# Attention scores in blocks of 32 queries from two heads, with 32, 64, 96 and 128 keys, in place of blocks of 64 queries with 64 and 128 keys

## The chip, the cores and the metric

The kernel runs on one core of one Trainium2 chip. A core has five engines with queues of their own: TensorE (PE in the profile; its weight loads are listed apart as PEld), VectorE (DVE), ScalarE (ACT), GpSimd (POOL) and SyncE (SP, which here only starts DMAs). The metric is the device time of one execution in microseconds (us), median of three runs.

## The reference: what is computed

A residual multi-query attention layer over 64 batches of 128 tokens, 16 heads of 64, causal, with one extra null key whose score is a learned bias:

```python
xn = layernorm(x, g_in)
q = (xn @ Wq).reshape(b, n, H, DH).transpose(0, 2, 1, 3) * scale
kv = xn @ Wkv                      # one key and one value head for all 16
...
sim = jnp.einsum('bhid,bjd->bhij', q, k) + bias
sim = jnp.where(causal_mask, neg, sim)
sim = jnp.where(mask_p[:, None, None, :], sim, neg)
attn = jax.nn.softmax(sim, axis=-1)
out = jnp.einsum('bhij,bjd->bhid', attn, v)
out = layernorm(out.transpose(0, 2, 1, 3).reshape(b, n, INNER) @ Wo, g_out)
return x + out
```

Everything is fp32. Because of the causal mask, a block of 32 queries needs only the keys up to its own block: the four blocks of a batch need 32, 64, 96 and 128 keys.

## The kernel before

**Layout.** The 128 tokens of a batch are cut into four blocks of 32 (`Q = 32`). `PLACE = 0, 1, 3, 2` (L98) gives the order in which the blocks are stored: blocks 0 and 1 form the first half of the queries (`hf = 0`), blocks 3 and 2 the second (`hf = 1`). Eight chunks of the query projection hold 16 heads, two of 64 in each chunk's 128 rows: a head is named by `r` (upper or lower 64 rows), `u` (chunks 0 to 3 or 4 to 7) and `f` (0 to 3).

**Scores.** `scores(b, hf)` (L765) computes the scores of one batch and one half of its queries. For each `f`, `r` and `u` it issues one matmul on a quarter of the array: the 64 rows of `r` against 64 of the array's columns. The weights are the 64 queries of one head, the moving operand is `kT`, the keys: 64 keys for `hf = 0`, 128 for `hf = 1`. The result goes to PSUM partitions `u * 64` to `u * 64 + 63`, so `u` picks the column half of the array. That is 16 matmuls for each half, and four of them (two `r`, two `u`) run side by side. An fp32 matmul appears in the trace as two records, called passes here. Keys past the causal edge inside the 64 or 128 are computed too, and are masked by the bias.

**Bias and mask.** `biasp` holds the bias of all heads in the layout of the scores, with a very negative number above the diagonal (`load_bias` L203, `causal` L215, `null_shift` L232, all of them in the setup). `bias_add` (L738, POOL) makes a tile `s` of bias plus key mask for a batch one turn ahead; `scores_add` (L790, DVE) then adds the scores out of PSUM to it, one instruction for each PSUM tile; `scores_max`, `exps` (ACT), `rinv` and `scale` (POOL) make the softmax, and `blocks_T` (DVE) transposes it in blocks of 32 for the next product.

**Values.** `values(b)` (L891) multiplies the transposed blocks with the values: eight tiles of 32 rows by 64 columns run side by side, `s` picking the 32 rows and `r` the columns. For the rows named in `wide` two steps of 128 columns are joined into one of 256, so that the tiles of odd `s` issue other lengths than those of even `s`.

**Order.** The order of the instructions on each engine is that of the source (`manual_schedule`); waits between engines are set from the tiles that they share. After a setup of some 60 us the main loop works on a pair of batches in each turn, `a = 2d` and `b = 2d + 1`: `turn(d)` (L1092) for d = 1 to 29 issues the four score groups (a,0), (b,0), (a,1), (b,1), then on DVE the adds of (a,0) and (b,0), a maximum, and the adds of (a,1) and (b,1); on PE the values of the pair before follow. Their four PSUM rooms are `a`, `w`, `Y` and the other `w`, which the adds of (a,0) and (b,0) have to free first. Then `body` or `body_full` issues the projections, the output product and the norms. The last turns use `turn_end` and `body_end` (d = 30, 31) and `body_last`.

**Other places that hold queries.** `qT` tiles are written by the helpers from L471 to L725 (`q_copy`, `keep`, `q_out`, `keep_two`, `q_out_two`, `inner_out`); before, 64 queries of a head lie side by side in them.

Of the kernel before, what the change touches and what calls it, by code (L numbers as in the profile page):

```python
# [8 lines left out]
FP = mybir.dt.float32  # L9
# [8 lines left out]
def kernel(  # L18
# [59 lines left out]
    nc = tc.nc  # L78
# [124 lines left out]
    def load_bias(u):  # L203
        rows = slice(u * DH, (u + 1) * DH)
        bias_r = attn_bias.rearrange("(u f r) i j -> u r i f j", u=2, r=2)[u]
        for r in range(2):
            rf = slice(r * NF, (r + 1) * NF)
            nc.sync.dma_start(out=biasp[rows, rf, LK], in_=bias_r[r, 0:DH, :, 0:NL])
            for i, at in enumerate((N - Q, N - 2 * Q)):
                nc.sync.dma_start(  # L210
                    out=biasp[u * DH + i * Q : u * DH + (i + 1) * Q, rf, UK],
                    in_=bias_r[r, at : at + Q],
                )

    def causal(u):  # L215

        for rows, keys, base in (
            (slice(u * DH, (u + 1) * DH), LK, 0),
            (slice(u * DH, u * DH + Q), UK, N - Q),
            (slice(u * DH + Q, (u + 1) * DH), UK, N - 2 * Q),  # L220
        ):
            nc.gpsimd.affine_select(
                biasp[rows, :, keys],
                biasp[rows, :, keys],
                pattern=[[0, R8], [-1, keys.stop - keys.start]],
                compare_op=ALU.is_ge,
                fill=NEG,
                base=base,
                channel_multiplier=1,
            )  # L230

    def null_shift(u):  # L232

        rows = slice(u * DH, (u + 1) * DH)
        nc.vector.tensor_copy(
            nbp[rows].rearrange("p (r f) -> p r f", r=2),
            nbh[rows, u * R8 : (u + 1) * R8].rearrange("p (f r) -> p r f", r=2),
        )
        nc.vector.tensor_tensor(
            biasp[rows, :, 1 : ROW - 1],  # L240
            biasp[rows, :, 1 : ROW - 1],
            nbp[rows].unsqueeze(2).broadcast_to([DH, R8, NL + N]),
            ALU.subtract,
        )
# [11 lines left out]
    nc.gpsimd.memset(biasp[0:DH], 0.0)  # L256
    nc.gpsimd.memset(biasp[DH:, :, 0 : ROW : ROW - 1], 0.0)
# [213 lines left out]
    def q_tiles(g, j, tags):  # L471

        for h, tag in enumerate(tags):
            qT[g, j, h] = gp.tile(
                [P, 2, GB // 2, 2, 2, DH], FP, tag=tag, name=f"qT_{g}_{j}_{h}", bufs=1
            )
            q_tags[g, j, h] = tag
# [4 lines left out]
    def q_part(g, c, h):  # L482

        f = c % NF
        return qT[g, f // 2, h][:, f % 2, :, :, c // NF, :]

    def q_whole(g, j, u, h):
        return qT[g, j, h][:, :, :, :, u, :]
# [18 lines left out]
    def q_copy(pq, c, h):  # L507
        nc.scalar.copy(
            q_part(0, c, h), pq.rearrange("p t (h i) -> p t h i", h=2)
        )  # L510
# [68 lines left out]
    def keep(tag, g, f, name):  # L579
        u, h = KEPT[name]  # L580
        nc.scalar.copy(
            q_part(g, u + f, h), prod[tag].rearrange("p (t h i) -> p t h i", t=2, h=2)
        )

    def q_out(g, c, h, tag, name=None):
        o = q_part(g, c, h)
        p = prod[tag].rearrange("p (t h i) -> p t h i", t=2, h=2)
# [24 lines left out]
    def keep_two(tag, g, j, name):  # L612
        u, h = KEPT[name]
        nc.scalar.copy(  # L614
            q_whole(g, j, u // HC, h).rearrange("p f t h i -> p (f t h) i"),
            prod[tag].rearrange("p f (n i) -> p (f n) i", i=DH),
        )

    def q_out_two(g, j, u, h, tag, name):
        v, k = KEPT[name]  # L620
        nc.vector.tensor_tensor(
            q_whole(g, j, u, h).rearrange("p f t h i -> p (f t h) i"),
            prod[tag].rearrange("p f (n i) -> p (f n) i", i=DH),
            q_whole(g, j, v // HC, k).rearrange("p f t h i -> p (f t h) i"),
            ALU.add,
        )
# [81 lines left out]
    def inner_out(k, g, h, part):  # L708

        u, hh = DEST[k]  # L710
        q = q_whole(g, h, u, hh)
        r = inner[k].rearrange("p a (h i) -> p a h i", h=2)
        four = q.rearrange("p f t h i -> p (f t) h i")
        o, p = {
            "00": (q[:, 0, 0], r[:, A0]),
            "01": (q[:, 0, 1], r[:, A0]),
            "11": (q[:, 1, 1], r[:, A0]),
            "00,11": (four[:, 0:4:3], r[:, A2 : A1 + 1]),
            "00 2": (q[:, 0, 0], r[:, A2]),
            "11 5": (q[:, 1, 1], r[:, A1]),  # L720
            "01,10": (four[:, 1:3], r[:, A1 : A0 + 1]),
            "1*": (q[:, 1], r[:, A0 : A0 + 1].broadcast_to([P, 2, 2, DH])),
            "*1": (q[:, :, 1], r[:, A1 : A1 + 1].broadcast_to([P, 2, 2, DH])),
        }[part]
        nc.vector.tensor_tensor(o, p, o, ALU.add)  # L725
# [39 lines left out]
    def scores(b, hf, tiles=None):  # L765
# [10 lines left out]
        for f in range(NF):  # L776
            for r in range(2):
                rows = slice(r * DH, (r + 1) * DH)
                for u in range(2):
                    nc.tensor.matmul(  # L780
                        home[r][u * DH : (u + 1) * DH, f, :],
                        qT[g, f // 2, t // 2][rows, f % 2, t % 2, hf, u],
                        kT[rows, 0 : nk // Q, t, :],
                        start=True,
                        stop=True,
                    )
# [3 lines left out]
    def scores_add(b, hf):  # L790
        sv = S[b][:, :, KEYS[hf]].rearrange("p (r f) j -> p r f j", r=2)
        pv = pss.pop((b, hf))
        if isinstance(pv, list):
            for r in (1, 0):
                nc.vector.tensor_tensor(sv[:, r], pv[r], sv[:, r], ALU.add)  # L795
        else:
            nc.vector.tensor_tensor(sv, pv, sv, ALU.add)
# [91 lines left out]
    WIDE = (1, 3)  # L889

    def values(b, wide=()):  # L891
# [8 lines left out]
        for turn in range(len(turns[0])):  # L900
            for s in range(NQ):
# [5 lines left out]
                quad = slice(s * Q, (s + 1) * Q)  # L907
                slots = slice(2 * to + j, 2 * to + j + 2 * n - 1, 2)
                for r in range(2):
# [8 lines left out]
                        tile_position=(s * Q, r * DH),  # L918
# [173 lines left out]
    def turn(d):  # L1092
# [28 lines left out]
    def turn_end(d):  # L1121
# [14 lines left out]
        scores(a, 0, ((ps_y, "Y"), (ps_w, "w")))  # L1136
        scores(b, 0, ((ps_q, "a"), (ps_w, "w")))
        scores(a, 1)
# [7 lines left out]
        scores(b, 1, ((ps_y, "Y"), (ps_q, "a")))  # L1146
# [572 lines left out]
    null_shift(1)  # L1719
# [7 lines left out]
    null_shift(0)  # L1727
# [8 lines left out]
    scores(0, 0, ((ps_y, "Y"), (ps_w, "w")))  # L1736
    scores(0, 1)
# [13 lines left out]
    scores(1, 0, ((ps_y, "X"), (ps_w, "w")))  # L1751
    scores(1, 1)
# [82 lines left out]
```

## Time and profile before

| | |
|---|---|
| runs | 1022.42, 1022.61, 1022.75 us; median 1022.61 |
| profiled execution | 1022.45 us, of it 1020.6 us span of the core |
| granted TensorE clock | 1.00 |
| busy | PE 1012.9 us, PEld 902.0, DVE 860.8, POOL 775.0, ACT 672.8 |
| one turn in the middle | 31.02 us (scores start at 527.34 and at 558.36) |
| of it scores, values | 2.84 us, 2.56 or 2.63 us |

The span is the time from the first to the last instruction of the core; what lies around it in the profiled execution is 1.85 us. PE's matmuls are pipelined, and a record's end is modelled, so how long a group of matmuls holds the engine is read from start to start. In the timeline rows the columns are start, duration, engine, line, operation, output<-inputs, size of the tile of the array (rows*columns), shape and count; a bracket gives the idle time before the row and what ended it.

### The profile page before, as it was taken

Reading aid. Unit: us, or ns where it says so; the run is one execution under the profiler, and the core shown is the slowest. Engines: PE = TensorE matmul, PEld = TensorE weight load, DVE = VectorE, ACT = ScalarE, POOL = GpSimd, SP = SyncE. Lnnn points to the kernel's source line nnn. Section 1 sums busy time; section 2 is a strip of 40 time slices with the busy share of each in tenths; the row PEclk is TensorE's granted clock in tenths of the full one; section 3 lists DMA queues with packets and bytes.
Section 4 is the critical chain, followed back from the end, with each engine's and each line's share of the span. In section 5 each row is a group of like instructions: output and inputs, shape, how many; then the busy total and the mean of one; then the engine's idle time right before and its main releaser. Section 6 shows DMA issues by size and latency. Waiting matters only on the chain.

```text
span 1020.6 us, 31143 instructions
## 1 busy us (share of the span) xinstructions
PE 1012.9 (99%) x12285; PEld 902.0 (88%) x12285; DVE 860.8 (84%) x1849; ACT 672.8 (66%) x2675; POOL 775.0 (76%) x621
## 2 busy tenths in 40 slices
PE   9999999999999999999999999999999999999997
PEld 9888888888888888888888888888888888888886
DVE  6877778888888988889888888888888888878787
ACT  5766677656677565686666776566765667856583
POOL 4997779678696876959768596785968769587686
PEclk9999999999999999999999999999999999999999
DMA  7415243151431425224152341514314152141221
GB/s 219 139 31 151 67 117 112 31 163 65 143 99 61 120 67 152 88 76 124 51 161 76 105 121 35 164 63 138 102 49 136 64 152 89 71 103 33 68 85 62
DMA packets 73833, 100.84 MB, mean 99 GB/s; under 512 B 32212, under 2 KB 36056, under 8 KB 71896
## 3 DMA queue, kind: packets, MB, share of 16 engines
q1 hardware_dynamic: 73392, 98.47, 32.3%
q8 instruction: 96, 1.57, 0.6%
q14 instruction: 49, 0.40, 0.1%
q10 hardware_dynamic: 296, 0.40, 0.1%
HBM read 63.19 MB, written 33.55 MB: 95 GB/s over the span
## 4 chain that ended last, share of the span: by engine, by line
PE 95%; ACT 2%; POOL 1%; DVE 1%; issue 0%; DMA 0%; POOLq 0%; DVEq 0%
PE pyX L998 20%; PE pa L603 13%; PE pi L697 11%; PE pyY L998 10%; PE po L911 8%; PE pkv L404 6%; PE pyw L998 5%; PE pc L603 4%; PE ps L780 3%; PE pq L499 3%; PE pa L554 2%; PE sc_X L780 2%; PE sc_Y L780 2%; PE pc L697 2%; ACT s L811 2%; PE pc L554 1%
## 5 line engine op out<-in xcount | busy, mean ns | idle before, releaser
L811 ACT ACTIVATE s<-s,nmax 128x65 f32<-128x65 f32 (+1 forms) x1024 | 370.9, 366 | 62.2 <-DVE nmax L802 62.2
L833 POOL TENSOR_TENSOR s<-s,rinv 128x512 f32<-128x512 f32 (+1 forms) x132 | 189.7, 1448 | 115.4 <-DVE rinv L829 112.9
L745 POOL TENSOR_TENSOR s<-biasp,mneg 128x1552 f32<-128x1552 f32 (+1 forms) x65 | 206.2, 3175 | 30.7 <-DVE s L795 21.2
L811 ACT ACTIVATION_READ_ACCUMULATOR s<-s,nmax 128x1 f32 x1024 | 194.5, 190 | 0.0
L725 DVE TENSOR_TENSOR qT<-pi,qT 128x128 f32<-128x128 f32 (+1 forms) x376 | 123.6, 340 | 35.9 <-PE pi L697 28.8
L1034 ACT COPY y<-pyX 128x256 f32<-128x256 f32 x29 | 10.8, 373 | 180.7 <-PE pyX L998 180.7
L802 DVE TENSOR_REDUCE nmax<-s 128x8 f32<-128x1032 f32 (+1 forms) x128 | 121.6, 950 | 0.1
L849 DVE STREAM_TRANSPOSE sb<-s 128x1536 f32<-128x1536 f32 (+1 forms) x68 | 113.6, 1674 | 2.1 <-POOL s L833 1.7
L998 PE MATMUL pyX<-wT,oT 128*128 128x256 f32 x464 | 109.7, 379 | 0.0
L998 PE MATMUL pyX<-wo,oT 128*128 128x256 f32 x464 | 109.7, 379 | 0.0
L978 POOL TENSOR_TENSOR oT<-oT 128x512 f32<-128x512 f32 x64 | 81.1, 1278 | 26.4 <-PE pyw L998 24.1
L998 PEld LDWEIGHTS pyX<-wT,oT 128*128 128x128 f32 x464 | 84.0, 190 | 9.2
L998 PEld LDWEIGHTS pyX<-wo,oT 128*128 128x128 f32 x464 | 84.0, 190 | 9.2
L911 PE MATMUL po<-sb,vr 32*64 32x128 f32 (+1 forms) x3700 | 86.2, 315 | 0.1
L911 PEld LDWEIGHTS po<-sb,vr 32*64 32x64 f32 x3700 | 74.8, 131 | 9.5 <-issue 5.3
L930 ACT ACTIVATE oT<-po,nv 128x512 f32<-128x512 f32 (+1 forms) x127 | 73.9, 660 | 0.4 <-PE po L911 0.4
L404 PE MATMUL pkv<-xT,wkv 128*128 128x256 f32 x256 | 63.3, 391 | 0.0
L998 PE MATMUL pyw<-wo,oT 128*128 128x256 f32 x256 | 60.5, 379 | 0.0
L998 PE MATMUL pyY<-wo,oT 128*128 128x256 f32 x256 | 60.5, 379 | 0.0
L998 PE MATMUL pyY<-wT,yS 128*128 128x256 f32 x256 | 60.5, 379 | 0.0
L614 ACT COPY qT<-pa 128x512 f32<-128x512 f32 x78 | 45.4, 582 | 17.7 <-PE pa L603 17.7
L404 PEld LDWEIGHTS pkv<-xT,wkv 128*128 128x128 f32 x256 | 46.2, 189 | 10.0 <-issue 4.8
(231 smaller groups left out, 2510.1 us busy)
## 6 DMA issues: line engine op xcount, KB each, us to landing
res<-in_x_dram SPq DMA_DIRECT2D x64, 256.0 KB
out_dram<-y SPq DMA_DIRECT2D x63, 256.0 KB
x<-in_x_dram SPq DMA_DIRECT2D x62, 256.0 KB
xd<-xb SPq DMA_DIRECT2D x14, 1024.0 KB
xT<-xd SPq DMA_DIRECT2D x56, 256.0 KB
vr<-vd SPq DMA_DIRECT2D x64, 128.0 KB
kT<-kT SPq DMA_DIRECT2D x32, 64.0 KB
vd<-vb SPq DMA_DIRECT2D x32, 64.0 KB
```

What stands on the lines that cost most here:

```text
L404: nc.tensor.matmul(pkv, wkv[:, kc, :], xT[g][:, t : t + 2, kc, :], start=(kc == 0), stop=(kc == KC - 1),)
L603: nc.tensor.matmul(prod[tag][:, i], w[:, kc, f * P : (f + 1) * P], t[:, :, kc, :], start=first, stop=(kc == HK - 1), skip_group_check=not ...
L697: nc.tensor.matmul(to, inner_w[k][i][:, h], inner_x[k, g][i], start=(i == 1), stop=True, skip_group_check=(i != 1),)
L725: nc.vector.tensor_tensor(o, p, o, ALU.add)
L745: nc.gpsimd.tensor_tensor(S[b][:, :, keys], biasp[:, :, keys], mneg[:, t, keys] .unsqueeze(1) .broadcast_to([P, R8, keys.stop - keys.start ...
L802: nc.vector.tensor_reduce(nmax[b][:, hf], S[b][:, :, WITH_NULL[hf]], AX.X, ALU.max, negate=True)
L811: nc.scalar.activation(row, row, AF.Exp, bias=nmax[b][:, hf, k : k + 1], accum_out=rsum[b][:, hf, k : k + 1],)
L833: nc.gpsimd.tensor_tensor(sv, sv, rinvs[b, hf][:, lo:hi].unsqueeze(2).broadcast_to([P, hi - lo, sv.shape[2]]), ALU.mult,)
L849: nc.vector.transpose(sbs[b][:, :, lo:hi].rearrange("p j e q -> p e j q"), S[b][:, lo:hi, 1 : ROW - 1].rearrange("p e (j k) -> p e j k", k=Q),
L911: nc.tensor.matmul(po[s][rows, to : to + n], vr[g][quad, t, PLACE[j], :], sb[quad, slots, r * NF : (r + 1) * NF, :], start=(turn == 0), st ...
L978: eng.tensor_tensor(o, a, b, op)
L998: nc.tensor.matmul(prod[key], h[:, c, :], w[:, c, :], start=(start and c == 0), stop=(c == HC - 1), skip_group_check=not start,)
```

## The change

The unit of a score matmul is now a block of 32 queries of the two heads `u = 0, 1` together (64 weight columns as before), and it takes only the keys that the block needs: 32, 64, 96 or 128. The column half of the array is picked by `i`, the block within the half, and no longer by `u`: column half 0 gets blocks 0 and 3 (32 and 128 keys), column half 1 blocks 1 and 2 (64 and 96 keys). The number of matmuls stays, 16 for each group. `scores_run` collects the matmuls of several groups and sorts them by the time at which their column half would come to them if a matmul took as long as it has blocks of keys.

The softmax tiles have their partitions in another order therefore: block, then head, where it was head, then block. `quarter`, `load_bias`, `causal`, `null_shift` and `values` (by `QUAD`) follow it. Where a block has fewer keys than the tile, the bias stays at the negative fill, and `scores_add` covers a PSUM tile in two instructions: all 128 partitions for the keys that both blocks have, and 64 partitions for the rest.

```diff
+    def quarter(u, i):
+        at = i * DH + u * Q
+        return slice(at, at + Q)
...
-        for f in range(NF):
-            for r in range(2):
-                rows = slice(r * DH, (r + 1) * DH)
-                for u in range(2):
-                    nc.tensor.matmul(
-                        home[r][u * DH : (u + 1) * DH, f, :],
-                        qT[g, f // 2, t // 2][rows, f % 2, t % 2, hf, u],
-                        kT[rows, 0 : nk // Q, t, :],
-                        start=True,
-                        stop=True,
-                    )
+        return home
+
+    def scores_run(*runs):
+
+        ready, todo = {}, []
+        for n, (b, hf, *tiles) in enumerate(runs):
+            g, t = divmod(b, GB)
+            home = scores(b, hf, *tiles)
+            for f in range(NF):
+                for i in range(2):
+                    blocks = key_blocks(hf, i)
+                    at = ready.get(i, 0)
+                    ready[i] = at + blocks
+                    for r in range(2):
+                        rows = slice(r * DH, (r + 1) * DH)
+                        todo.append(
+                            (
+                                at,
+                                n,
+                                f,
+                                r,
+                                i,
+                                home[r][i * DH : (i + 1) * DH, f, 0 : blocks * Q],
+                                qT[g, f // 2, t // 2][rows, f % 2, t % 2, hf, i],
+                                kT[rows, 0:blocks, t, :],
+                            )
+                        )
+        for *_, to, q, k in sorted(todo, key=lambda x: x[:5]):
+            nc.tensor.matmul(
+                to, q.rearrange("p u q -> p (u q)"), k, start=True, stop=True
+            )
+
+    def key_blocks(hf, i):
+        return 1 + (PLACE[2 * hf + i])
...
         pv = pss.pop((b, hf))
+        few, many = sorted(key_blocks(hf, i) for i in range(2))
+        more = slice(0, DH) if key_blocks(hf, 0) == many else slice(DH, P)
+        parts = (slice(0, P), slice(0, few * Q)), (more, slice(few * Q, many * Q))
         if isinstance(pv, list):
             for r in (1, 0):
-                nc.vector.tensor_tensor(sv[:, r], pv[r], sv[:, r], ALU.add)
+                for at, keys in parts:
+                    o = sv[at, r, :, keys]
+                    nc.vector.tensor_tensor(o, pv[r][at, :, keys], o, ALU.add)
         else:
-            nc.vector.tensor_tensor(sv, pv, sv, ALU.add)
+            for at, keys in parts:
+                o = sv[at, :, :, keys]
+                nc.vector.tensor_tensor(o, pv[at, :, :, keys], o, ALU.add)
...
     WIDE = (1, 3)
+    QUAD = 0, 2, 1, 3
...
-                quad = slice(s * Q, (s + 1) * Q)
+                at = QUAD[s] * Q
+                quad = slice(at, at + Q)
...
-                        tile_position=(s * Q, r * DH),
+                        tile_position=(at, r * DH),
...
-        scores(a, 0, (homes[0], (ps_w, "w")))
-        scores(b, 0, (homes[1], (ps_w, "w")))
-        scores(a, 1)
-        scores(b, 1, ((ps_y, "X"), (ps_q, "c")))
+        scores_run(
+            (a, 0, (homes[0], (ps_w, "w"))),
+            (b, 0, (homes[1], (ps_w, "w"))),
+            (a, 1),
+            (b, 1, ((ps_y, "X"), (ps_q, "c"))),
+        )
```

In the same way `turn_end` makes one run of (a,0), (b,0), (a,1) and one of (b,1), and the setup one run for each of the batches 0 and 1. The setup's bias work is cut differently: 16 DMAs of 32 queries where there were 12, eight `causal` selects on 32 partitions by 8 heads by 32 keys where there were six larger ones, one `null_shift` over all partitions where there were two over 64, and a memset of 256 elements for each half of the partitions where one of 1552 elements filled half of them. The writers of `qT` split their last index from 64 queries into 2 by 32.

**On PE, the turn d = 4 (batches 8 and 9), from its first score matmul on, before.** `sc_0_Y` and `sc_0_w` are the PSUM tiles of batch a, half 0, for the two `r`; `qT` holds the queries, `kT` the keys; the shape is 64 rows by the number of keys:

```order
L780 MATMUL sc_0_Y<-kT,qT_0_0_1308 64x64 x2
L780 MATMUL sc_0_w<-kT,qT_0_0_1308 64x64 x2
L780 MATMUL sc_0_Y<-kT,qT_0_0_1308 64x64 x2
L780 MATMUL sc_0_w<-kT,qT_0_0_1308 64x64 x2
L780 MATMUL sc_0_Y<-kT,qT_1_0_1693 64x64 x2
L780 MATMUL sc_0_w<-kT,qT_1_0_1693 64x64 x2
L780 MATMUL sc_0_Y<-kT,qT_1_0_1693 64x64 x2
L780 MATMUL sc_0_w<-kT,qT_1_0_1693 64x64 x2
L780 MATMUL sc_0_a<-kT,qT_0_0_1308 64x64 x2
```

Four matmuls of one length (two rows here) go to the four quarters of the array at a time, and batch b (`sc_0_a`) follows when batch a is through. The same place with the change:

```order
L812 MATMUL sc_0_Y<-kT,qT_0_0_1340 64x32
L812 MATMUL sc_0_Y<-kT,qT_0_0_1340 64x64
L812 MATMUL sc_0_w<-kT,qT_0_0_1340 64x32
L812 MATMUL sc_0_w<-kT,qT_0_0_1340 64x64
L812 MATMUL sc_0_Y<-kT,qT_0_0_1340 64x32
L812 MATMUL sc_0_w<-kT,qT_0_0_1340 64x32
L812 MATMUL sc_0_Y<-kT,qT_0_0_1340 64x64
L812 MATMUL sc_0_w<-kT,qT_0_0_1340 64x64
L812 MATMUL sc_0_Y<-kT,qT_1_0_1732 64x32
L812 MATMUL sc_0_w<-kT,qT_1_0_1732 64x32
L812 MATMUL sc_0_Y<-kT,qT_1_0_1732 64x32
L812 MATMUL sc_0_w<-kT,qT_1_0_1732 64x32
```

Column half 0 (32 keys) gets two matmuls of each `r` for one of column half 1 (64 keys); further on 32-key matmuls of batch b come ahead of the last 64-key ones of batch a, and 128-key ones (`hf = 1`) ahead of the last 64-key ones of batch b.

**On DVE, the adds of the same turn, before.** `s_1677` is the softmax tile of batch a, `s_1896` that of batch b:

```order
L795 TENSOR_TENSOR s_1677<-sc_0_w,s_1677 128x4x64
L795 TENSOR_TENSOR s_1677<-sc_0_Y,s_1677 128x4x64
L795 TENSOR_TENSOR s_1896<-sc_0_w,s_1896 128x4x64
L795 TENSOR_TENSOR s_1896<-sc_0_a,s_1896 128x4x64
L802 TENSOR_REDUCE nmax_1998<-s_1677 128x8
L797 TENSOR_TENSOR s_1677<-ps_1_1959,s_1677 128x8x128
L795 TENSOR_TENSOR s_1896<-sc_1_c,s_1896 128x4x128
L795 TENSOR_TENSOR s_1896<-sc_1_X,s_1896 128x4x128
```

And with the change, up to the adds of (a,1):

```order
L831 TENSOR_TENSOR s_1716<-sc_0_w,s_1716 128x4x32
L831 TENSOR_TENSOR s_1716<-sc_0_w,s_1716 64x4x32
L831 TENSOR_TENSOR s_1716<-sc_0_Y,s_1716 128x4x32
L831 TENSOR_TENSOR s_1716<-sc_0_Y,s_1716 64x4x32
L831 TENSOR_TENSOR s_1935<-sc_0_w,s_1935 128x4x32
L831 TENSOR_TENSOR s_1935<-sc_0_w,s_1935 64x4x32
L831 TENSOR_TENSOR s_1935<-sc_0_a,s_1935 128x4x32
L831 TENSOR_TENSOR s_1935<-sc_0_a,s_1935 64x4x32
L840 TENSOR_REDUCE nmax_2041<-s_1716 128x8
L835 TENSOR_TENSOR s_1716<-ps_1_1966,s_1716 128x8x96
L835 TENSOR_TENSOR s_1716<-ps_1_1966,s_1716 64x8x32
```

Every add is now two, with the same number of elements in a partition together; the four adds ahead of the maximum have become eight, and seven adds of a turn fourteen.

More of the change, by code (lines that the diff above doesn't have):

```diff
@@ L207, in load_bias @@
             rf = slice(r * NF, (r + 1) * NF)
[L208 to L212, printed above, removed]
-                )
[L215 to L229, printed above, removed]
-            )
@@ L232, in null_shift @@
[L232 to L238, printed above, removed]
+            for hf, keys in ((0, LK), (1, UK)):
+                for i in range(2):
+                    block = PLACE[2 * hf + i]
+                    nk = (block + 1) * Q
+                    nc.sync.dma_start(
+                        out=biasp[quarter(u, i), rf, keys.start : keys.start + nk],
+                        in_=bias_r[r, block * Q : (block + 1) * Q, :, 0:nk],
+                    )
@@ new lines, in quarter, with causal @@
+    def quarter(u, i):
+        at = i * DH + u * Q
+        return slice(at, at + Q)
+    def causal(u):
+        for hf, keys in ((0, LK), (1, UK)):
+            for i in range(2):
+                at = keys.start + PLACE[2 * hf + i] * Q
+                own = biasp[quarter(u, i), :, at : at + Q]
+                nc.gpsimd.affine_select(
+                    own,
+                    own,
+                    pattern=[[0, R8], [-1, Q]],
+                    compare_op=ALU.is_ge,
+                    fill=NEG,
+                    base=0,
+                    channel_multiplier=1,
+                )
@@ L239, in null_shift @@
+    def null_shift():
+        for u in range(2):
+            for i in range(2):
+                rows = quarter(u, i)
+                nc.vector.tensor_copy(
+                    nbp[rows].rearrange("p (r f) -> p r f", r=2),
+                    nbh[rows, u * R8 : (u + 1) * R8].rearrange("p (f r) -> p r f", r=2),
+                )
         nc.vector.tensor_tensor(
-            biasp[rows, :, 1 : ROW - 1],
-            biasp[rows, :, 1 : ROW - 1],
-            nbp[rows].unsqueeze(2).broadcast_to([DH, R8, NL + N]),
+            biasp[:, :, 1 : ROW - 1],
+            biasp[:, :, 1 : ROW - 1],
+            nbp.unsqueeze(2).broadcast_to([P, R8, NL + N]),
@@ L1135, in turn_end @@
             return
-        scores(a, 0, ((ps_y, "Y"), (ps_w, "w")))
-        scores(b, 0, ((ps_q, "a"), (ps_w, "w")))
-        scores(a, 1)
+        scores_run(
+            (a, 0, ((ps_y, "Y"), (ps_w, "w"))),
+            (b, 0, ((ps_q, "a"), (ps_w, "w"))),
+            (a, 1),
+        )
         scores_add(a, 0)
@@ L1718 @@
     norm_T(4)
-    null_shift(1)
     causal(0)
```

51 lines of the change are left out of this document (26 added, 25 removed).

## The prediction

> **What bounds the kernel.** First the busy shares and the chain of work that ended last, on the page, then the waits of PE over the whole span:
>
> ```profile
> PE 1012.9 (99%) x12285; PEld 902.0 (88%) x12285; DVE 860.8 (84%) x1849; ACT 672.8 (66%) x2675; POOL 775.0 (76%) x621
> ...
> PE 95%; ACT 2%; POOL 1%; DVE 1%; issue 0%; DMA 0%; POOLq 0%; DVEq 0%
> ```
>
> ```profile
> PE busy L1667 <- POOL neg L255: 1.4, 1, 1.4
> PE pyc L998 <- DVE y L1032: 0.6, 1, 0.6
> ```
>
> PE is the chain, and its only waits that the profile names lie at the start and at the end. So a turn lasts as long as its matmuls hold PE, and the change is worth what it takes from or adds to PE, as long as no other engine becomes late. A busy share of 99% is no proof of a full pace, therefore I read the pace from start to start. The timeline of all engines at the scores of one turn (rows of matmuls and weight loads), and three places with other shapes:
>
> ```profile
> 527.34 0.27 PE L780 MATMUL sc_Y<-kT,qT 64*64 64x64 f32 x2
> ...
> 527.45 0.23 PE L780 MATMUL sc_Y<-kT,qT 64*64 64x64 f32 x2
> ...
> 527.45 0.14 PEld L780 LDWEIGHTS sc_Y<-kT,qT 64*64 64x64 f32 x2
> ...
> 527.51 0.23 PE L780 MATMUL sc_Y<-kT,qT 64*64 64x64 f32 x2
> 527.51 0.14 PEld L780 LDWEIGHTS sc_Y<-kT,qT 64*64 64x64 f32 x2
> ```
>
> ```profile
> 528.32 1.06 PE L780 MATMUL ps<-kT,qT 64*64 64x128 f32 x32
> 529.20 0.28 PE L780 MATMUL sc_X<-kT,qT 64*64 64x128 f32 x2
> ...
> 530.18 2.63 PE L911 MATMUL po<-sb,vr 32*64 32x256 f32 x116
> ```
>
> ```profile
> 507.24 1.89 PE L603 MATMUL pa<-xS,wS 128*128 128x256 f32 x8
> 508.97 1.89 PE L603 MATMUL pc<-xS,wS 128*128 128x256 f32 x8
> ```
>
> ```profile
> 8.88 5.52 PE L499 MATMUL pq<-xT,wq 128*128 128x128 f32 x48
> 14.24 1.04 PE L354 MATMUL pxT<-wR,x 128*128 128x128 f32 x8
> ```
>
> The scores of a turn take 530.18 - 527.34 = 2.84 us. The 64-key groups (a,0) and (b,0) are 16 passes deep on each quarter of the array; from the second pass (527.45) to the first 128-key one (528.32) are 15 of them, 58 ns each. The 128-key group has 32 records on four quarters, 8 deep: 0.88 / 8 = 110 ns.
>
> **The change, step by step.** (1) *Keys streamed.* Before, each column half of the array streams, for each f and r, 64 + 128 keys; after it is 32 + 128 on half 0 and 64 + 96 on half 1, five blocks where there were six. If time went by keys alone, a sixth of the stage would go. Does a pass of 32 keys take half of one of 64? No row shows fewer keys than weight columns, so I bound it. **Lower end:** 256 keys take 1.73 / 8 = 216 ns and 128 keys 110, so 128 keys cost 106 to 107 ns and a pass about 3 more; 32 keys by keys alone: 27 + 3 = 30 ns. **Upper end:** the weights of a pass still are 64 columns. The weight load of the next pass starts when a pass starts (527.45 and 527.51 in both kinds of rows), so it sees the next pass 58 ns later. By keys alone a 64-key pass would be 53 + 3 = 56; it takes 58. With 128 weight columns and 128 keys (the setup's projections) it is 5.36 / 48 = 112 ns, where 64 columns and 128 keys take 110. Both small excesses appear where there are as many weight columns as keys, and there the weight load ends last. A 32-key pass with 64 weight columns then takes 58 ns too. I take the upper end, 58: it is the row with the same weights.
>
> The Trainium skill's page "TensorE: Matmul & The Clock Gate", section "LDWEIGHTS (loading the stationary operand)", has loading time go by the columns alone, columns / 1.2 in ns, some 53 ns for 64; the 58 ns rows agree with it. Its section "Back-to-back issue gap" lets matmuls of up to 64 columns go at a floor of about 25 ns, which taken alone would give the first rival below. The page "TensorEngine Tiling (Array Packing)", section "Instruction Overhead", has a matmul of one column last as long as one of 60 and warns against cutting a dimension that is small already; by it the sum would be an estimated 1.7 us lower.
>
> With 58 ns, half 0 takes 16 x 58 + 16 x 110 in a turn, exactly as before. Half 1 takes 16 x 58 + 16 x 83 (96 keys: 80 + 3) and finishes early, which helps nobody, since the values need both halves. Term: 0 in each of the 29 turns, between -0.43 us (both halves at five blocks) and the loss of step 2.
>
> (2) *Out of step.* Before, four equal matmuls start together. Do unequal ones disturb each other? The nearest rows are the values stage in three turns, in the windows view (with the values' line as filter; the columns are the stretch, its length, then the busy time and the count of PE and of weight loads, clock, DMA):
>
> ```profile
> 126.36:128.81 2.45, 2.45 (x128) 2.20 (x128) 1.00 0.02 7
> 157.58:160.14 2.56, 2.56 (x116) 2.30 (x116) 1.00 0.29 93
> 188.60:191.23 2.63, 2.63 (x112) 2.38 (x112) 1.00 0.03 6
> ```
>
> The first has equal lengths on all tiles; in the others joined steps put rows out of step, with fewer records and the same columns, and they last 0.11 and 0.18 us longer. So being out of step can cost up to 0.18. I take 0 for the scores: they have four tiles, not eight, and half 0, which sets the end, is never behind half 1 in the sorted order. The values themselves change only the rows that a tile sits on: 0.
>
> (3) *DVE's adds.* The timeline of DVE in the same turn:
>
> ```profile
> 528.10 0.43 DVE L795 TENSOR_TENSOR s<-sc_w,s 128x256 f32<-128x256 f32 x1 [0.28 <-PE sc_w L780]
> 528.45 0.41 DVE L795 TENSOR_TENSOR s<-sc_Y,s 128x256 f32<-128x256 f32 x1
> 528.78 0.41 DVE L795 TENSOR_TENSOR s<-sc_w,s 128x256 f32<-128x256 f32 x1
> 529.11 0.41 DVE L795 TENSOR_TENSOR s<-sc_a,s 128x256 f32<-128x256 f32 x1
> 529.44 0.68 DVE L802 TENSOR_REDUCE nmax<-s 128x8 f32<-128x520 f32 x1
> 530.04 1.21 DVE L797 TENSOR_TENSOR s<-ps,s 128x1024 f32<-128x1024 f32 x1
> 531.17 0.68 DVE L795 TENSOR_TENSOR s<-sc_c,s 128x512 f32<-128x512 f32 x1
> 531.77 0.68 DVE L795 TENSOR_TENSOR s<-sc_X,s 128x512 f32<-128x512 f32 x1
> 532.37 0.68 DVE L802 TENSOR_REDUCE nmax<-s 128x8 f32<-128x520 f32 x1
> ```
>
> From start to start 256 elements take 0.33 us, 512 take 0.60, 1024 take 1.13: 0.07 for the instruction and 1.04 ns for an element. Seven more instructions cost 7 x 0.065 = 0.45 us of DVE in a turn, 0.26 of it ahead of the maximum (eight of 0.20 in place of four of 0.33). What hides it: the values wait for room `a`, freed by the last of these adds, now done at 529.52; with the change at 528.10 + 1.39 + 0.28 = 529.77, at most 0.23 later if the last 64-key matmuls of batch a queue behind five 32-key ones. PE comes at 530.18, so 0.2 to 0.4 us are left. The next in line is ACT, whose exps start when the maximum is done and which then empties the rooms of the values:
>
> ```profile
> 530.16 0.35 ACT L811 ACTIVATE s<-s,nmax 128x65 f32<-128x65 f32 x1 [2.34 <-DVE nmax L802]
> ...
> 532.83 2.41 ACT L930 ACTIVATE oT<-po,nv 128x512 f32<-128x512 f32 x4
> ```
>
> ```profile
> 534.57 1.89 PE L603 MATMUL pa<-xT,wq 128*128 128x256 f32 x8
> ```
>
> PE takes room `a` again at 534.57, while ACT empties it first, by 532.83 + 0.6 = 533.43: 1.1 us of cover for at most 0.5 us of delay. Term in the 29 turns: 0.
>
> (4) *The end.* In `turn_end` the rooms `w` are what the values wait for, and DVE comes late there:
>
> ```profile
> 982.36 3.15 PE L911 MATMUL po<-sb,vr 32*64 32x256 f32 x128
> ```
>
> ```profile
> 982.65 0.41 DVE L795 TENSOR_TENSOR s<-sc_w,s 128x256 f32<-128x256 f32 x1
> ...
> 998.68 1.91 DVE L849 STREAM_TRANSPOSE sb<-s 128x768 f32<-128x768 f32 x2
> ```
>
> The second `w` is freed at 983.06, 0.7 us after PE's first value matmul; six adds of 0.20 in place of three of 0.33 make it 0.2 us later, in two turns: +0.4. In the last turn no later PE work covers the chain maximum, exps, scaling, transposes (till 1000.59), so DVE's 0.45 us come through: +0.45.
>
> (5) *Setup.* The bias work shrinks on POOL and DVE, with four more DMAs; PE, which has no named wait there but for its first instruction, gains nothing: 0. The writers of `qT` keep their elements, in runs of 32: 0.
>
> **Sum.** 1022.45 us (the profiled execution, 1020.6 of span and 1.85 around it) + 0 + 0 + 0.4 + 0.45 = 1023.3. That execution is 0.16 below the median of the runs, 1022.61; on their scale it is **1023.5 us**, 0.1% above.
>
> **Rivals.** *Time goes by keys (faster).* If a 32-key pass takes 30 ns, half 1 bounds the stage and 16 x (110 - 83) = 0.43 us go from each turn. Then PE comes to the values at 529.75, just as the last add ends (529.77, and its hand-over); 0.1 us is given back, 0.33 x 29 = 9.6 us remain, and two setup runs give 0.2 each: 1013.4, between 1008 and 1018. Against it stand the 58 and 112 ns.
>
> *Out of step costs (slower).* If the scores pay what the values pay, 0.11 to 0.18 in 29 turns are 3.2 to 5.2 us: 1026.7 to 1028.7. For it, the three windows; against it, the smaller number of tiles.
>
> *The values wait for the adds (slower).* Place: PE's first value matmul, room `a`. It decides when the eight adds end after 530.1, with a spacing above 0.24 us in place of 0.20. The mean of the nearest DVE row of 128 elements from PSUM, its whole duration, is 0.28:
>
> ```profile
> L725 DVE TENSOR_TENSOR qT<-pi,qT 128x128 f32<-128x128 f32 x218 | 61.1, 281 | 26.3 <-PE pi L697 22.4 <-ACT qT L614 0.2
> ```
>
> At that spacing they end at 530.35, and 0.25 x 29 = 7.3 us make it 1030.8. Against it: DVE's instructions overlap from one to the next in all rows above. The Trainium skill's page "TensorEngine Tiling (Array Packing)", section "PSUM Bottleneck", names this very risk, that emptying PSUM becomes the limit when matmuls are packed; the 0.66 us between 529.52 and 530.18 say that it has not yet here.
>
> **Chances.** No gain and no loss in the turns: 0.55. Out of step costs: 0.17. The adds are waited for: 0.13. Time goes by keys: 0.12. Anything else 0.03, mostly slower. A measurement of this kernel tells about 0.2%, 2 us, from no change: faster by more 0.13, within it 0.55, slower 0.32. The likeliest case by itself spans 1022 to 1025. The range takes in both slower rivals and a small gain from 32-key passes, 1019 to 1031; it leaves out the full gain by keys and the far ends.
>
> **What would show it.** Score starts from row to row: 58 ns between 32-key passes on one quarter confirms step 1, 30 refutes it. The stage from its first matmul to the first value matmul: 2.84 unchanged, 2.95 to 3.02 if out of step costs, 2.4 to 2.5 in the fast case. PE's waits: a new one on DVE's line of adds at the values means the third rival. DVE's adds 0.20 us apart confirm step 3. I am wrong if the weight load of a pass does not set its pace, or if a later engine, fed 0.3 to 0.5 us late in each turn, holds PE at a place that I gave no price.

## The result, and the profile after

| | before | with the change |
|---|---|---|
| median of the runs | 1022.75 us (1022.42 to 1023.49) | 1054.15 us (1053.75 to 1054.45) |
| span of the profiled execution | 1020.6 us | 1052.4 us |
| granted TensorE clock | 1.00 | 0.998 |
| one turn, mean of 20 in the middle | 31.05 us | 32.06 us |
| scores: first to last matmul start | 2.642 us | 2.635 us |
| first score matmul to first add of DVE | 0.76 us | 0.97 us |
| first score matmul to first value matmul | 2.84 us | 3.57 us (even d), 3.53 us (odd d) |
| values, first start to the next work | 2.56, 2.63 us | 2.56, 2.63 us |

The change makes the kernel slower: ratio 1.0305, 95% interval 1.029 to 1.032. All four rows of stages are worked out from starts of matmuls and adds, as medians over the turns in the middle. Scores and values hold PE as long as before, and most of the lost time lies between them. The busy shares and the chain on the page of the changed kernel:

```profile
PE 1023.6 (97%) x12285; PEld 904.8 (86%) x12285; DVE 896.0 (85%) x2073; ACT 668.1 (63%) x2675; POOL 768.9 (73%) x624
...
PE 87%; DVE 7%; ACT 2%; issue 2%; POOL 1%; POOLq 0%; DVEq 0%
```

DVE, 1% of the chain before, now has 7%. The waits of PE and of its weight loads (group, what it waited for: us in all, times, longest):

```profile
PE po L951 <- DVE s L831: 9.9, 15, 0.7
PE po L951 <- PE sc_c L812: 8.7, 14, 0.6
...
PEld po L951 <- PE sc_c L812: 24.0, 28, 0.9
PEld pi L705 <- DVE qT L733: 5.2, 12, 0.4
PEld pi L705 <- POOL xI L685: 3.9, 9, 0.4
```

Two waits are new. In 28 of the 29 full turns the first value matmul (`po`) waits; in the first of them, d = 1, a later value matmul does, and the stage of the values is 0.74 us longer. (The 29th wait in the view's two lines is in a `turn_end`.) The view names DVE's adds in one half of the turns and PE itself in the other half, although PE's last score matmul had ended 0.62 us before. The matmul starts about 0.15 us after the last add's end where DVE is named (even d), and 0.10 us after it where PE is named (odd d), so the adds are the cause in both. From the fourth turn on, two of the inner products of the projections (`pi`) wait too in every other turn, one for DVE and one for POOL. One turn on DVE, and PE's first value matmul in it:

```profile
544.38 0.60 DVE L831 TENSOR_TENSOR s<-sc_w,s 128x128 f32<-128x128 f32 x2 [0.48 <-PE sc_w L812]
545.00 0.60 DVE L831 TENSOR_TENSOR s<-sc_Y,s 128x128 f32<-128x128 f32 x2
545.62 0.60 DVE L831 TENSOR_TENSOR s<-sc_w,s 128x128 f32<-128x128 f32 x2
546.24 0.60 DVE L831 TENSOR_TENSOR s<-sc_a,s 128x128 f32<-128x128 f32 x2
546.87 0.69 DVE L840 TENSOR_REDUCE nmax<-s 128x8 f32<-128x520 f32 x1
547.59 1.28 DVE L835 TENSOR_TENSOR s<-ps,s 128x768 f32<-128x768 f32 x2
548.80 0.74 DVE L831 TENSOR_TENSOR s<-sc_c,s 128x384 f32<-128x384 f32 x2
549.46 0.74 DVE L831 TENSOR_TENSOR s<-sc_X,s 128x384 f32<-128x384 f32 x2
```

```profile
546.98 0.43 PE L951 MATMUL po<-sb,vr 32*64 32x256 f32 x2 [0.67 <-DVE s L831]
```

Each row of adds is a pair: one of 128 partitions, then one of 64. Ahead of the maximum a pair takes 0.62 us from start to start (544.38, 545.00, 545.62, 546.24), 0.31 for an add, where 0.20 was forecast. Behind the maximum a pair of 384 and 128 elements takes 0.66 us (548.80 to 549.46), just 0.46 + 0.20. So a 128-element add is worth 0.31 us at one place and 0.20 at another. What differs is where the 64-partition add starts: ahead of the maximum at partition 64, behind it at partition 0. The seams show it too. The pair of `sc_a` ends at 546.84, the maximum starts 0.03 us after that; it ends at 547.56, and the next add starts 0.03 after that. In the rows of before that the prediction quotes, DVE's next add or maximum started 0.08 us before the end of the one in front.

### The profile page after: what moved, and what is told of

It is laid out like the page before. It is cut to its first block, busy times and chain, and to the rows that moved or that the text cites. A ratio compares the mean times of both kernels' runs of the same rounds, so it can differ in the third digit from the quotient of the medians.

```text
span 1052.4 us, 31407 instructions
## 1 busy us (share of the span) xinstructions
PE 1023.6 (97%) x12285; PEld 904.8 (86%) x12285; DVE 896.0 (85%) x2073; ACT 668.1 (63%) x2675; POOL 768.9 (73%) x624
## 4 chain that ended last, share of the span: by engine, by line
PE 87%; DVE 7%; ACT 2%; issue 2%; POOL 1%; POOLq 0%; DVEq 0%
PE pyX L1038 19%; PE pa L611 13%; PE pi L705 11%; PE pyY L1038 10%; PE po L951 7%; PE pkv L411 5%; PE pyw L1038 5%; PE pc L611 4%; DVE s L831 4%; PE pq L507 3%; ACT s L849 2%; PE pa L562 2%; PE pc L705 2%; PE sc_Y L812 1%; PE ps L812 1%
## 5 line engine op out<-in xcount | busy, mean ns | idle before, releaser
L849 ACT ACTIVATION_READ_ACCUMULATOR s<-s,nmax 128x1 f32 x1024 | 196.7, 192 | 0.0
L951 PEld LDWEIGHTS po<-sb,vr 32*64 32x64 f32 x3700 | 78.3, 131 | 28.9 <-PE sc_c L812 24.0
L831 DVE TENSOR_TENSOR s<-sc_w,s 128x128 f32<-128x128 f32 (+1 forms) x128 | 37.4, 292 | 22.5 <-PE sc_w L812 20.7
```

The source lines that it names most:

```text
L849: nc.scalar.activation(row, row, AF.Exp, bias=nmax[b][:, hf, k : k + 1], accum_out=rsum[b][:, hf, k : k + 1],)
L951: nc.tensor.matmul(po[s][rows, to : to + n], vr[g][quad, t, PLACE[j], :], sb[quad, slots, r * NF : (r + 1) * NF, :], start=(turn == 0), st ...
```

## The experiments

**The theories.** H, a hold: an instruction of DVE whose operands start at another partition than those of the one in front begins only when that one has ended. S, short adds: two short adds out of PSUM in a row take 0.31 us each, wherever they start. Beside them, that the order of the matmuls or the 96-key blocks cost the time. The table gathers the runs. "First value" is the first value matmul after the first score matmul, mean of even and odd d. "Maximum" is the start of a turn's first maximum, and "second" that of its second, both against that value matmul; all are medians, in us. These last two columns are for odd d; where PE waits at the values, both are 0.05 us earlier in even d.

| run | time | ratio (95%) | first value | maximum | second |
|---|---|---|---|---|---|
| before | | | 2.84 | -0.74 | 2.18 |
| the change | 1054.15 | 1.0305 (1.029 to 1.032) | 3.55 | -0.07 | 3.19 |
| k64 | 1023.46 | 1.0003 (0.9994 to 1.0012) | 2.83 | -0.74 | 2.39 |
| k64_split | 1024.84 | 1.0015 (1.0006 to 1.0025) | 2.83 | -0.48 | 2.64 |
| pairs | 1041.9 | 1.018 (1.0165 to 1.0196) | 3.13 | -0.07 | 3.19 |
| fours | 1046.1 | 1.0223 (1.0208 to 1.0239) | 3.31 | -0.07 | 3.19 |
| flip | 1038.14 | 1.0148 (1.0133 to 1.0164) | 2.84 | -0.27 | 3.52 |
| plain | 1047.5 | 1.0241 (1.0225 to 1.0256) | 3.33 | -0.07 | 3.18 |
| red0 | 1023.32 | 1.0003 (0.9994 to 1.0012) | 2.84 | -0.44 | 2.49 |
| red64 | 1044.37 | 1.0207 (1.019 to 1.0224) | 3.25 | 0.11 | 3.05 |
| late | 1027.08 | 1.0041 (1.0026 to 1.0055) | 2.84 | -0.08 | 2.85 |

**k64: whole adds again.** Block 0 gets 64 keys; its bias keeps the negative fill for the 32 that are added.

```diff
     def key_blocks(hf, i):
-        return 1 + (PLACE[2 * hf + i])
+        return 1 + PLACE[2 * hf + i] if hf else 2
...
+        if few == many:
+            parts = parts[:1]
```

> Block 0 gets 64 keys in place of 32 (its bias keeps the negative fill there), so that the four adds ahead of the maximum are whole again, 128x256 each as before the change; order by columns and the 128 and 96 keys of the other half stay. Theory H (an add that starts at another partition than the add in front of it begins only when that one has ended; 0.31 us from start to start in place of 0.20) and theory S (two short adds out of PSUM in a row take 0.31 us each wherever they start): no named wait of PE at the values, 1022 to 1025 us. If the loss hangs on the order of the matmuls or on the 96-key blocks instead: 1040 us or more. If a 32-key pass were cheaper than a 64-key pass, the scores would last up to 0.4 us longer than the changed kernel's 2.64 us from first to last start; by the weight loads they stay within 0.03 us.

1023.46 us, no wait at the values. The 96-key blocks, their order beside the 128-key ones and the cut adds behind the maximum are still in it, so these cost next to nothing by themselves. The loss hangs on what is left out: the 32-key blocks, with the order that they bring, and the cut adds ahead of the maximum. The scores last 2.635 us from first to last start with 32 keys and with 64: a 32-key pass with 64 weight columns is no cheaper.

**k64_split: eight adds, all from partition 0.**

```diff
-        parts = (slice(0, P), slice(0, few * Q)), (more, slice(few * Q, many * Q))
+        parts = (slice(0, P), slice(0, few * Q)), (more, slice(few * Q, many * Q))
+        if few == many:
+            parts = (slice(0, P), slice(0, Q)), (slice(0, P), slice(Q, 2 * Q))
```

> As the run with 64 keys for block 0, but each of the four adds ahead of the maximum is cut into two of 128x128, both from partition 0: eight adds with 128 elements each, as in the changed kernel. H: 0.20 us from start to start, the last add ends 0.3 us later than with four, hidden; 1022 to 1026 us. S: 0.31 us from start to start, PE waits about 0.45 us for them in each turn; 1037 to 1050 us.

The run fell to H, with 1024.84 us. DVE in one turn of it:

```profile
529.06 0.49 DVE L833 TENSOR_TENSOR s<-sc_w,s 128x128 f32<-128x128 f32 x2 [0.27 <-PE sc_w L812]
529.46 0.48 DVE L833 TENSOR_TENSOR s<-sc_Y,s 128x128 f32<-128x128 f32 x2
529.86 0.47 DVE L833 TENSOR_TENSOR s<-sc_w,s 128x128 f32<-128x128 f32 x2
530.25 0.47 DVE L833 TENSOR_TENSOR s<-sc_a,s 128x128 f32<-128x128 f32 x2
530.65 0.68 DVE L842 TENSOR_REDUCE nmax<-s 128x8 f32<-128x520 f32 x1
```

As many adds, as short, in as many instructions as with the change, and a pair takes 0.40 us in place of 0.62: 0.20 for an add. S is out.

**pairs and fours: fewer switches.** Both are the changed kernel with its adds in another order. In `pairs` the two of 128 partitions of a batch come ahead of its two of 64 partitions; in `fours` this goes for both batches together.

```diff
-            for r in (1, 0):
-                for at, keys in parts:
+            for at, keys in parts:
+                for r in (1, 0):
```

> The changed kernel with its adds in another order: for each batch first the two of 128 partitions, then the two of 64 partitions that start at partition 64. H: four spacings of 0.31 to 0.33 us and four of 0.20 us, 2.05 us in all in place of 2.49; PE's wait at the values falls from 0.71 to about 0.27 us and the time to 1032 to 1042 us. S: nothing changes, 1053 to 1056 us.

> The changed kernel with all four adds of 128 partitions of both batches ahead of the four of 64 partitions. H: two long spacings are left, 1.81 us in all; PE waits 0 to 0.1 us at the values; 1023 to 1034 us. S: nothing changes, 1053 to 1056 us.

`pairs` came as H has it: 2.07 us for the eight adds, PE's first value at 3.13 in place of 3.55, 1041.9 us. `fours` missed its range, 1046.1 us, in spite of only two switches:

```profile
508.84 0.29 DVE L832 TENSOR_TENSOR s<-sc_w,s 128x128 f32<-128x128 f32 x1 [0.48 <-PE sc_w L812]
509.05 0.28 DVE L832 TENSOR_TENSOR s<-sc_Y,s 128x128 f32<-128x128 f32 x1
509.64 0.29 DVE L832 TENSOR_TENSOR s<-sc_w,s 128x128 f32<-128x128 f32 x1 [0.31 <-PE sc_w L812]
509.85 0.28 DVE L832 TENSOR_TENSOR s<-sc_a,s 128x128 f32<-128x128 f32 x1
510.14 0.29 DVE L832 TENSOR_TENSOR s<-sc_w,s 64x128 f32<-64x128 f32 x1
510.36 0.29 DVE L832 TENSOR_TENSOR s<-sc_Y,s 64x128 f32<-64x128 f32 x1
```

The third add, first of batch b, comes too early for PE, whose matmuls for it are not through, and DVE stands 0.31 us. The spacings are as H has them (0.29 at the switch, about 0.21 after it), and two adds in a row that both start at partition 64 are 0.22 us apart (510.14 to 510.36): the upper half by itself is not slow. The expectation had forgotten whose result an earlier add waits for.

**flip: the column halves change places.** With `PLACE = 1, 0, 2, 3` blocks 1 and 2 sit on column half 0, blocks 0 and 3 on half 1. The lists that follow from it in the copies of the keys, the values and their output are turned too; nothing else changes.

```diff
-    PLACE = 0, 1, 3, 2
+    PLACE = 1, 0, 2, 3
...
-    WIDE = (1, 3)
+    WIDE = (0, 2)
```

> The column halves change places: blocks 1 and 2 (64 and 96 keys) go to column half 0, blocks 0 and 3 (32 and 128 keys) to half 1, in scores, bias and values alike; computation, number and size of the matmuls and of the adds stay. Now the 64-partition adds ahead of the maximum start at partition 0, and those of the second half of the queries at partition 64. H: the eight adds ahead of the maximum stand 0.20 us apart, PE's wait at the values is gone; the six adds behind the maximum and the second maximum are held instead, some 0.6 us in all, where PE does not wait: 1024 to 1036 us. S: the eight stay at 0.31 us: 1052 to 1056 us.

```profile
536.76 0.48 DVE L831 TENSOR_TENSOR s<-sc_w,s 128x128 f32<-128x128 f32 x2 [0.49 <-PE sc_w L812]
537.16 0.47 DVE L831 TENSOR_TENSOR s<-sc_Y,s 128x128 f32<-128x128 f32 x2
...
538.95 1.38 DVE L835 TENSOR_TENSOR s<-ps,s 128x768 f32<-128x768 f32 x2
540.37 0.87 DVE L831 TENSOR_TENSOR s<-sc_c,s 128x384 f32<-128x384 f32 x2
541.25 0.56 DVE L831 TENSOR_TENSOR s<-sc_X,s 128x384 f32<-128x384 f32 x1
```

The slow adds moved with the start partition: ahead of the maximum a pair now takes 0.40 us, behind it 0.88 (540.37 to 541.25) in place of 0.66. PE's wait at the values is gone, as forecast. The time, 1038.14, is 2 us above the range, and about as much of it is not the adds' at all: with the rows of `WIDE` turned, the values take 2.65 and 2.69 us in place of 2.63 and 2.56. The rest of the loss, some 12 us, lies in the projections and the output product behind them, so work that is late behind the maximum takes up the range to its end.

**plain: without the sorting.**

```diff
-sorted(todo, key=lambda x: x[:5])
+sorted(todo, key=lambda x: x[1:5])
```

> The changed kernel without its sorting: the matmuls of one batch and half are through before the next ones start, the column halves in step. If the sorted order is worth time on PE, the scores last longer than 2.64 us from first to last start. If it only puts the last 64-key matmuls of the first batch behind 32-key ones of the second, the first add starts 0.76 us after the first score matmul in place of 0.97, PE's wait at the values falls from 0.71 to 0.5 us, and the time to 1046 to 1050 us.

1047.5 us, as expected for the second case. The scores last 2.635 us either way, so the sorted order gains PE nothing. It delays DVE's first add from 0.75 to 0.97 us, and since PE waits for the adds, that is 6.7 us of the whole time.

**tiny0 and tiny64: a small add between the adds of before.** 64 partitions, 8 elements, from partition 0 or from 64. `tiny` is a tile of zeros; `tiny64` and `red64` take `tiny[DH:]` where the cuts shown have `tiny[0:DH]`.

```diff
                 nc.vector.tensor_tensor(sv[:, r], pv[r], sv[:, r], ALU.add)
+                if hf == 0:
+                    z = tiny[0:DH]
+                    nc.vector.tensor_tensor(z[:, 0], z[:, 1], z[:, 2], ALU.add)
```

> The kernel before the change, with a small add of its own data behind each of the four adds ahead of the maximum: 64 partitions from partition 0, 8 elements each. H and S: four times about 0.08 us, hidden as the four extra adds of the run with eight adds from partition 0 were; 1022 to 1025 us.

> The same with the small add on partitions 64 to 127. H: each small add waits for the end of the add in front of it, and the next add for the end of the small one, 0.60 to 0.65 us from add to add in place of 0.33; the last add ends some 3.0 us after the first score matmul, PE waits 0.25 to 0.4 us at the values and loses some 0.3 us later in the turn; 1034 to 1046 us. Without a hold by the start partition: as from partition 0, 1022 to 1025 us.

Both missed by far, 1171.92 and 1181.53 us, and tell nothing of the start partition, since something else took over. DVE and POOL in one turn of `tiny0`:

```profile
426.00 0.41 DVE L797 TENSOR_TENSOR s<-sc_w,s 128x256 f32<-128x256 f32 x1
426.33 2.88 DVE L800 TENSOR_TENSOR tiny<-tiny 64x8 f32<-64x8 f32 x1
...
425.99 3.21 POOL L747 TENSOR_TENSOR s<-biasp,mneg 128x1552 f32<-128x1552 f32 x1 [1.54 <-ACT mneg L734]
```

An add of 8 elements lasts 2.88 us and ends at 429.21; POOL's add of 1552 elements, which began 0.34 us before it, ends at 429.20. With both inputs in SBUF the small add stood until POOL's instruction was through.

**red0 and red64: the same with one input.** A small maximum in place of the small add.

```diff
-                    nc.vector.tensor_tensor(z[:, 0], z[:, 1], z[:, 2], ALU.add)
+                    nc.vector.tensor_reduce(z[:, 0, 0:2], z[:, 1:3], AX.X, ALU.max)
```

> The kernel before the change, with a small maximum of its own data behind each of the four adds ahead of the maximum: one input of 2x8 elements in SBUF, on 64 partitions from partition 0. One input only, since the small add with two inputs from SBUF took up to 2.9 us beside GpSimd's work and told nothing. H and a loss by mere count: from add to add about 0.41 us in place of 0.33, hidden; 1022 to 1025 us.

> The same small maximum on partitions 64 to 127. H: it starts when the add in front has ended, and the next add when it has ended, 0.60 to 0.65 us from add to add; the last add ends about 3.0 us after the first score matmul, PE waits 0.25 to 0.4 us at the values and loses about 0.3 us later in the turn; 1034 to 1046 us. Without a hold by the start partition: as from partition 0, 1022 to 1025 us.

First a turn of `red0`, then one of `red64`:

```profile
528.60 0.43 DVE L797 TENSOR_TENSOR s<-sc_w,s 128x256 f32<-128x256 f32 x1 [0.27 <-PE sc_w L782]
528.94 0.15 DVE L800 TENSOR_REDUCE tiny<-tiny 64x2 f32<-64x16 f32 x1
529.02 0.41 DVE L797 TENSOR_TENSOR s<-sc_Y,s 128x256 f32<-128x256 f32 x1
```

```profile
539.97 0.43 DVE L797 TENSOR_TENSOR s<-sc_w,s 128x256 f32<-128x256 f32 x1 [0.27 <-PE sc_w L782]
540.41 0.17 DVE L800 TENSOR_REDUCE tiny<-tiny 64x2 f32<-64x16 f32 x1
540.61 0.43 DVE L797 TENSOR_TENSOR s<-sc_Y,s 128x256 f32<-128x256 f32 x1
```

The same instructions on the same number of partitions of the kernel before; only the first partition differs. From add to add it is 0.42 us from partition 0 and 0.64 us from partition 64, and the kernel takes 1023.32 and 1044.37 us. H is shown without any of the change's other parts.

**late: DVE late behind the adds, no hold.** Four small maxima in a chain ahead of the first maximum of the kernel before.

```diff
         scores_add(b, 0)
+        z = tiny[0:DH]
+        for _ in range(4):
+            nc.vector.tensor_reduce(z[:, 0, 0:2], z[:, 1:3], AX.X, ALU.max)
         scores_max(a, 0)
```

> The kernel before the change, with four small maxima of their own data (partitions 0 to 63, each waits for the one in front) between the adds of the two batches and the first maximum of a turn: the rooms of the values are freed as early as before, but DVE's work from the maximum on comes some 0.67 us later, about as late against PE as in the changed kernel. If the second part of the loss, some 0.3 us in a turn, comes from this lateness alone: no wait at the values, waits of PE at the inner products of the projections (pi) in every other turn, 1028 to 1034 us. If it hangs on the wait at the values or on the held adds: 1022 to 1025 us.

1027.08 us, a little under the range: the mechanism is there, but half as large. The waits of the weight loads in it have one of the two lines of `pi`:

```profile
PEld pi L699 <- DVE qT L727: 5.2, 12, 0.4
```

The one for POOL is missing. To see what each is worth I compared the starts of PE's matmuls one by one with those of a kernel without the loss (before for the change, `late` and `red64`, `k64` for `flip` and `k64_split`), and summed the delay that each group newly shows, in us over the whole execution:

| run | second maximum against the first value | late at `pi<-xS` (waits for DVE) | late at `pi<-xI` (waits for POOL) |
|---|---|---|---|
| k64_split | 2.64 | 0.6 | 0 |
| late | 2.85 | 3.6 | 0 |
| red64 | 3.05 | 3.4 | 1.8 |
| the change | 3.19 | 3.6 | 3.0 |
| flip | 3.52 | 3.4 | 4.5 |

`flip` loses another 1.7 us at the output product (`pyY<-wT,yS`). The later DVE is with the second maximum, the more is lost: first at the room that DVE empties, later at POOL's sums. In `late` it is 0.34 us earlier than with the change, which is why that run has the first part of the loss alone. That the lateness goes by way of the second maximum is read from this order of five runs; no run delayed POOL by itself.

## Why the prediction was wrong

The forecast was 1023.5 us, no change, with 1019 to 1031 as the range; it is 1054.15.

*Scores of a turn: right.* A 32-key pass takes 58 ns from start to start on a quarter of the array, the end of the bounds that I took, and the scores stage is 0.007 us shorter. Three of these passes in a row on one quarter, with the change:

```profile
543.49 0.22 PE L812 MATMUL sc_Y<-kT,qT 64*64 64x32 f32 x1
...
543.55 0.22 PE L812 MATMUL sc_Y<-kT,qT 64*64 64x32 f32 x1
...
543.61 0.22 PE L812 MATMUL sc_Y<-kT,qT 64*64 64x32 f32 x1
```

With 64 keys in place of 32 (k64) it stays. The rivals "time goes by keys" and "out of step costs" did not happen; the values kept their 2.56 and 2.63 us.

*The first add: right.* "At most 0.23 later" for 64-key matmuls that queue behind 32-key ones; it is 0.21, and `plain` takes it back.

*DVE's adds: wrong, and this is the step that failed.* "Eight of 0.20 in place of four of 0.33", 0.26 us more ahead of the maximum, hidden by 0.2 to 0.4 us of margin. The spacing of 0.07 us and 1.04 ns for an element is right for adds that start at the same partition (`k64_split`: 0.20). I carried it over to adds that go to and fro between partition 0 and partition 64, where each begins only when the one in front has ended: 0.31. So the eight take 2.49 us from first start to the maximum in place of 1.6.

The third rival, that the values wait for the adds at room `a`, is what happened. It had the place and the point from which it decides ("a spacing above 0.24 us"), but a price of 0.25 us for a turn, from a spacing of 0.28 and no delay of the first add. With the measured terms the same sum gives: first add 0.21 later, seven spacings of 0.31 and a last duration of 0.29 end 3.43 us after the first score matmul, and PE follows 0.12 later at 3.55, 0.71 behind the 2.84 of before. That is the largest term: 29 x 0.71 = 20.6 us, and the sum turn by turn, with the 0.74 us inside the values of d = 1, gives the same.

*The cover behind the adds: wrong too.* I had "1.1 us of cover for at most 0.5 us of delay", read at room `a` and ACT. DVE's first maximum now comes 0.67 us later against PE, its second 1.0 us, and the inner products of the next projections have less cover than that: 3.6 + 3.0 = 6.6 us over the execution. The prediction named this as a way to be wrong (a later engine "at a place that I gave no price").

*The end: half right.* Each `turn_end` was to lose 0.2 us. From the first value matmul to the next work it takes 3.69 and 3.86 us in place of 2.89 and 3.08, 0.8 more, by the same held adds. The last turn, from its first value matmul to the end of the span, grew from 21.84 to 22.32 us, 0.48 where 0.45 was forecast. *Setup:* the first turn's scores start at 60.53 us in place of 60.35, near the 0 of the forecast.

The terms add up: 20.6 + 6.6 + 1.6 + 0.5 + 0.2 = 29.5 of the 31.8 us by which the span grew. Of the rest, 1.8 us are single delays at `pa` and `pc` in the first two turns of the main loop (103 to 139 us); 0.5 us are not placed.

**A row of before that I passed over.** The adds that I took the 0.07 us from all start at partition 0. But DVE also transposes the value tile there, which lies on partitions 64 to 127 (L442), once in every other turn:

```profile
518.08 0.62 DVE L725 TENSOR_TENSOR qT<-pi,qT 128x256 f32<-128x256 f32 x2 [0.15 <-PE pi L697]
518.74 0.71 DVE L442 STREAM_TRANSPOSE vb<-vT 64x512 f32<-64x512 f32 x1
```

The transpose starts 0.03 us after the end at 518.70, and its instruction has no wait, while all adds that I quoted overlap by 0.08. That it is a transpose does not explain it: those of the other tiles, which start at partition 0, overlap too. One of them:

```profile
494.64 0.42 DVE L725 TENSOR_TENSOR qT<-pi,qT 128x256 f32<-128x256 f32 x1
494.98 1.77 DVE L849 STREAM_TRANSPOSE sb<-s 128x1536 f32<-128x1536 f32 x1
```

It starts 0.08 us before the end at 495.06. So the row at 518.74 shows the same hold, and it was in the trace before the change.

The Trainium skill's page "VectorE: DVE Perf Modes", section "Two Vector instructions with no wait between them", gives it as a model: an instruction whose input or output starts in another group of 32 partitions than the last one of that memory is held until all earlier ones have finished. The trace agrees to the detail: the add at 547.59 is held although the maximum in front of it starts at partition 0, because the last instruction that read PSUM, an add of `sc_a`, had started at 64. Only starts at 0 and at 64 were compared here; groups of 32 are what the page states. The prediction weighed pages on TensorE and not this one.

**What stays open.** No version beat the kernel before; `k64` equals it, since the half with 32 or 64 and 128 keys still sets the end of the scores. Placing every second batch the other way round would make the halves equal and the scores, by an estimate from the passes of 128 and 96 keys 8 x 27 ns = 0.22 us shorter in each turn, as long as PE doesn't wait for the adds; it needs a second bias tile and was not tried.

## What to carry to other kernels

Before a DVE instruction is cut in two, look at the first partition of each piece: pieces that start at the same partition cost 0.07 us each, pieces that change it also lose the overlap, 0.11 us at every change. Price an instruction from rows that are followed by the same kind of neighbour, and look for the one row whose seam differs. Where an engine is a few tenths of a microsecond ahead of the bound, count the cover at every later place that it feeds, not only at the next one.

## What the runs showed of the hardware

An add on DVE with both inputs in SBUF, 8 elements on 64 partitions, stood 2.88 us until POOL's add was through, to within 0.01 us. The same add with POOL idle took 0.15 us, and the maximum with one input (`red0`) was not stopped beside the same add of POOL: 0.15 us. A held add also lasts about 0.02 us longer itself: with 384 elements 0.56 us in `flip`, where it is held, and 0.54 with the change, where it is not; for adds of 128 elements this is less clear, 0.29 held and 0.27 to 0.29 not.
